# Narrow key tiles of an attention kernel: scores for weights and for maxima of four heads together, in two halves of the same banks

## The chip, the cores and the metric

The kernel runs on one core of one Trainium2 chip. The metric is the device time of one execution in microseconds, as the median of several runs; a profile of one execution is read beside it.

## The reference

The reference is one transformer block on x of 4 x 1024 x 512 (fp32): a layer norm, attention with 16 heads of 32, a layer norm of its output added to x, and then a gated feed-forward net with integer weights, again with a layer norm before and behind it and added.

```python
kqv = x @ Wqkv + bqkv                       # q, k, v: 16 heads of 32
scores = jnp.einsum('bsnh,btnh->bnst', k, q) / math.sqrt(HEAD_SIZE)
ones = jnp.ones_like(scores)
scores = jnp.triu(scores) + -10000.0 * jnp.tril(ones, k=-1)
attn = jax.nn.softmax(scores, axis=2)
out = jnp.einsum('bnkq,bknh->bqnh', attn, v)
out = out.reshape(b, s, NUM_HEADS * HEAD_SIZE)
return out @ Wo + bo

x = x + _layernorm(_L0_attn_ref(_layernorm(x), ...))
x = x + _layernorm(_L0_ffn_ref(_layernorm(x), ...))   # (silu(h Wg) * (h Wu)) Wd
```

For each query the softmax needs a maximum over the keys, the exponentials of the scores less that maximum, their sum, and their product with v.

## The kernel before, in words

The attention stage takes 1250 of the 1980 us; the feed-forward stage (`ffn`) follows and is not touched.

Attention runs in steps (b, hb, g): the batch b of 4, the block hb of four heads, and the half g of 512 queries. A step has 4(g + 1) key tiles of 128 keys. Each key tile c is one period of the main loop, 192 in all, and in a period two things stand side by side:

- `weights(now, c, halves)` makes the scores of 128 keys (the partitions) against the queries that may see them: a product of three rows with ones (L346, it takes the maximum off) and a product of k and q over 32 partitions for each head (L354). ScalarE takes the exponential (L371), POOL sets the diagonal block to zero (L373). The columns n are 512 for most c; in the last key tiles of a step, c = 4g + 1, 4g + 2 and 4g + 3, they are 384, 256 and 128.
- `maxima(unit, jj, k, halves)` makes, for the step that comes 12 periods later (LEAD), the scores of 128 queries (the partitions) against up to 512 keys, over again and the other way round (L265). VectorE limits the diagonal block (L273, "the mask") and takes the maximum (L277, "the reduction"). In the periods with c = 4g + 2 and 4g + 3 these have 256 and 128 columns too.

A half is two heads. A head of 32 takes one of the four groups of 32 rows of the array, so that two heads of weights and the other two heads of maxima run at the same time. That is the order before: in each period, for u = 0 and u = 1, `weights` of half u and `maxima` of half 1 - u.

[...] The pool `ps_st` holds one tile of two banks (one half of weights), `ps_big` is a ring of two tiles of two banks, and `ps_acc` holds `po` and `pd` (outputs and denominators). The ring `ps_big` serves the maxima, and all other work on TensorE that is put between: the projections of q, k and v (`pq`, L237), the output projection (`py`, L237), transposes (`xt` L461, `pv` L488, `pm` L301) and the masked part (`pb` L313). A tile of the ring can be used again when the tile two places before it has been emptied.

Between the two halves of a period stand, on TensorE, `values` of the key tile before (`po` and `pd`, L390) and a piece of other work: `fill_whole` (one of `xt`, `pv`, `pm`, `pb`, where one is due), or else `fill` (one `pq` or `py`). At the end of a period `fill` may add one or more. How much is filled is planned by costs and due times, and the plan is not changed by the edit. Where g = 1, the denominators of the first five key tiles are added up by a DMA that accumulates (L417); `pd` uses the sum in c = 6 and 7.

The order on every engine is the one in which the code issues the instructions (manual_schedule), and waits are set for tiles that are read or written. In the last 12 periods no maxima are left, and `weights` is called with both halves at once; in the first 12 no weights, and `maxima` with both.

```python
pool, tag = (ps_big, "big") if u and len(halves) > 1 else (ps_st, "st")   # weights
...
for u in range(2):                                                        # main loop
    if now and (unit or u == 0):
        weights(*now, [u] if unit else range(2))
    if unit and now:
        maxima(*unit, [1 - u])
```

Of the kernel before, what the change touches and what calls it, by code (L numbers as in the profile page):

```python
# [27 lines left out]
def tile_attn_ffn_sandwich(  # L28
# [70 lines left out]
    with ExitStack() as actx:  # L99
# [143 lines left out]
                    )  # L243


        def maxima(step, jj, k, halves, alone=False):


            b, hb, g = step
            if ("nm", step) not in state:  # L250
                state["nm", step] = e3.tile(
                    [P, 2, 4, HPB], F32, tag="nm", name=f"nm_{b}_{hb}_{g}"
                )
            nm = state["nm", step]
            qT, kT = state["q", b, hb], state["k", b, hb]
            j = 4 * g + jj
            n = min((j + 1) * P - 512 * k, 512)
            for u in halves:
                pool, tag = (ps_st, "st") if alone and u else (ps_big, "big")
                sc = pool.tile(  # L260
                    [P, 2, 512], F32, tag=tag,
                    name=f"sc_{b}_{hb}_{j}_{k}_{u}",
                )
                for h in (2 * u, 2 * u + 1):
                    nc.tensor.matmul(  # L265
                        sc[:, h % 2, :n],
                        lhsT=qT[h * D : (h + 1) * D, ts(j, P)],
                        rhs=kT[h * D : (h + 1) * D, 512 * k : 512 * k + n],
                        start=True,
                        stop=True,  # L270
                    )
                if k == g:
                    nc.vector.tensor_tensor(  # L273
                        sc[:, :, n - P : n], sc[:, :, n - P : n],
                        bound.unsqueeze(1).to_broadcast((P, 2, P)), ALU.min,
                    )
                nc.vector.tensor_reduce(  # L277
                    nm[:, k, jj, 2 * u : 2 * u + 2], sc[:, :, :n], AX.X, ALU.max, negate=True
                )
# [50 lines left out]
            later.extend((counts, shared))  # L330
            state["extra", step] = t1, t2

        def weights(step, c, halves):


            b, hb, g = step
            qT, kT, mT = state["q", b, hb], state["k", b, hb], state["mT", step]
            q0 = max(c * P, 512 * g)
            n = 512 * (g + 1) - q0
            st = {}  # L340
            for u in halves:
                pool, tag = (ps_big, "big") if u and len(halves) > 1 else (ps_st, "st")
                st[u] = pool.tile([P, 2, 512], F32, tag=tag, name=f"st_{b}_{hb}_{g}_{c}_{u}")
            heads = [h for u in halves for h in (2 * u, 2 * u + 1)]
            for h in heads:
                nc.tensor.matmul(  # L346
                    st[h // 2][:, h % 2, :n],
                    lhsT=ones_bf[h * D : h * D + 3, :],
                    rhs=mT[h * D : h * D + 3, 512 - n :],
                    start=True,  # L350
                    stop=False,
                )
            for h in heads:
                nc.tensor.matmul(  # L354
                    st[h // 2][:, h % 2, :n],
                    lhsT=kT[h * D : (h + 1) * D, ts(c, P)],
                    rhs=qT[h * D : (h + 1) * D, q0 : q0 + n],
                    start=False,
                    stop=True,
                )  # L360
            for u in halves:


                to_sum = g > 0 and c == 0
                pT = (p2 if to_sum else ppt).tile(
                    [P, 2, 512], F32, tag="sum" if to_sum else "pT",
                    name=f"pT_{b}_{hb}_{g}_{c}_{u}",
                )
                if to_sum:
                    state["sum", step, u] = pT  # L370
                nc.scalar.activation(pT[:, :, :n], st[u][:, :, :n], AF.Exp)  # L371
                if c >= 4 * g:
                    nc.gpsimd.affine_select(  # L373
                        out=pT[:, :, :P], in_=pT[:, :, :P], compare_op=ALU.is_ge, fill=0.0,
                        base=0, pattern=[[0, 2], [1, P]], channel_multiplier=-1,
                    )
                state["pT", step, c, u] = pT
# [36 lines left out]
        def add_up(step, c, u):  # L414

            if 0 < c <= 4 * step[2]:
                nc.gpsimd.dma_start(  # L417
                    state["sum", step, u], state["pT", step, c, u], accum_op=ALU.add
                )

        def finish(step):
            b, hb, g = step
            if g == 0:
                state["o", b, hb] = (p2 if hb < HC - 1 else p1).tile(
                    [P, S], F32, tag=f"o{hb}", name=f"o_{b}_{hb}"
                )
            o = state["o", b, hb]
            t1, t2 = state.pop(("extra", step))
            nc.vector.tensor_tensor(t2, state["pd"], t2, ALU.add)
            nc.vector.tensor_tensor(t1, state["po"], t1, ALU.add)  # L430

            def divide(k):
                nc.vector.reciprocal(t2[:, ts(k, P)], t2[:, ts(k, P)])  # L433
                nc.gpsimd.tensor_tensor(  # L434
                    o[:, ts(4 * g + k, P)], t1[:, ts(k, P)], t2[:, ts(k, P)], ALU.mult
                )

            for k in range(4):
                later.append(lambda k=k: divide(k))
# [168 lines left out]
        def put(lane, cost, due, ready, f, *args):  # L608
            lane.append((cost, due, ready, f, args))
# [72 lines left out]
        def rate(p):  # L682

            may = sorted(w[:2][::-1] for lane in lanes.values() for w in lane if w[2](p))
            got = total = 0.0
            for due, cost in may:
                total += cost
                got = max(got, total / max(due + 1 - p, 1))

            if p < at[1, 0, 0] - 4:  # L690
                return got
            left = sum(w[0] for lane in lanes.values() for w in lane if w[1] < n_periods)
            return max(got, left / max(n_periods - p, 1))
# [14 lines left out]
        def fill_whole(p):  # L708
            ahead = heads(whole, p)
            if ahead:  # L710
                piece(whole[ahead[0][1]])
            return bool(ahead)
# [21 lines left out]
        for p in range(-LEAD, n_periods + 1):  # L734
            unit = units[p + LEAD] if p + LEAD < len(units) else None
            now = tiles[p] if 0 <= p < n_periods else None
            before = tiles[p - 1] if p >= 1 else None
            spare[0] = max(spare[0], -FULL / 2) + rate(p)
            if rest:
                rest.pop(0)()  # L740
            for u in range(2):
                if now and (unit or u == 0):

                    weights(*now, [u] if unit else range(2))
                if unit and now:
                    maxima(*unit, [1 - u])
                elif unit and u == 0:
                    maxima(*unit, range(2), alone=True)
                if later:
                    later.pop(0)()  # L750
                if before:
                    add_up(*before, u)
                if u == 0:
                    if before:
                        values(*before)
                        if before[1] == 4 * before[0][2] + 3:
                            finish(before[0])

                    if not fill_whole(p) and (
                        not now or now[1] - 4 * now[0][2] > 1 or spare[0] > 1.5 * FULL  # L760
                    ):
                        fill(p, 1)
            if unit and unit[1:] == (0, unit[0][2]):
                shift_parts(unit[0])
                put(whole["rows"], 0, p, lambda q, p=p: q > p, shift_rows, unit[0])
            if now and now[1] == 1:
                put(whole["rows"], 0, p + 1, lambda q, p=p: q > p, masked_part, now[0])
            fill(p, 9)
            if p >= 0 and p % 4 != 3:
                n = next(looks, None)  # L770
                if n is not None:
                    look(n)
            if p > at[B - 1, HC - 1, 0] - LEAD and not pre and not (lanes["qk"] or lanes["v"]):
                ffn_begin()
                for i in range(GT + 1):
                    put(whole["ln"], 0, n_periods, lambda q, t=p + 3 + i: q >= t, ffn_stage, i)
                put(whole["ln"], 0, n_periods, lambda q: True, check_weights)
# [271 lines left out]
```

## Time and profile before

| | |
|---|---|
| median of 3 runs | 1982.24 us (1980.31 to 1984.41) |
| profiled execution | 1981.68 us, span 1979.9 us, granted clock 0.993 |
| TensorE busy | 1888.3 us |
| VectorE busy | 1159.2 us |
| ScalarE busy | 644.2 us |
| POOL busy | 529.3 us |
| L265, scores for maxima | 1536 matmuls, 346.5 us busy |
| L354 and L346, scores for weights | 1536 and 768 matmuls, 307.8 and 125.6 us |
| L277 and L273, maxima and masks | 384 and 256, 367.0 and 109.7 us |
| L371, exponentials | 384, 310.6 us |

Busy times of one line are the union of its instructions, so matmuls that run side by side count once. PE is TensorE, PEld its loading of weights, DVE VectorE, ACT ScalarE. An fp32 matmul of the program shows as two records (two passes), one of bf16 as one. The time that ends in "<-" names what the engine waited for before the instruction.

### The profile page before, as it was taken

Reading aid. Unit: us, or ns where it says so; the run is one execution under the profiler, and the core shown is the slowest. Engines: PE = TensorE matmul, PEld = TensorE weight load, DVE = VectorE, ACT = ScalarE, POOL = GpSimd, SP = SyncE. Lnnn points to the kernel's source line nnn. Section 1 sums busy time; section 2 is a strip of 40 time slices with the busy share of each in tenths; the row PEclk is TensorE's granted clock in tenths of the full one; section 3 lists DMA queues with packets and bytes.
Section 4 is the critical chain, followed back from the end, with each engine's and each line's share of the span. In section 5 each row is a group of like instructions: output and inputs, shape, how many; then the busy total and the mean of one; then the engine's idle time right before and its main releaser. Section 6 shows DMA issues by size and latency. Waiting matters only on the chain.

```text
span 1979.9 us, 42013 instructions
## 1 busy us (share of the span) xinstructions
PE 1888.3 (95%) x18209; PEld 1119.2 (57%) x18209; DVE 1159.2 (59%) x1903; ACT 644.2 (33%) x962; POOL 529.3 (27%) x908
## 2 busy tenths in 40 slices
PE   7999999899999999999999988999999999999997
PEld 4434434444444444444444433688888888888886
DVE  4678767677666676666666773554443444444444
ACT  2234434334333334333344323122222222222221
POOL 2133333243344244244233255201010101101011
PEclk9999999999999999999999999999999999999999
DMA  3163354264154153153244266431010101001000
GB/s 113 54 145 77 85 119 100 67 150 84 36 107 102 34 113 75 34 118 87 38 86 81 82 150 140 156 121 43 1 43 1 43 0 43 27 17 43 1 22 23
DMA packets 66784, 141.74 MB, mean 72 GB/s; under 512 B 6432, under 2 KB 20768, under 8 KB 66592
## 3 DMA queue, kind: packets, MB, share of 16 engines
q0 software_dynamic: 18432, 67.12, 18.2%
q1 hardware_dynamic: 41008, 67.40, 10.2%
q10 hardware_dynamic: 7152, 4.46, 0.8%
q8 instruction: 145, 2.38, 0.5%
q14 instruction: 47, 0.39, 0.1%
HBM read 55.07 MB, written 16.78 MB: 36 GB/s over the span
## 4 chain that ended last, share of the span: by engine, by line
PE 49%; DVE 3%; DMA 2%; POOL 1%; ACT 1%; issue 1%; POOLq 0%; DVEq 0%
PE pg L891 12%; PE pu L891 12%; PE acc L924 12%; PE pq L237 3%; PE py L237 3%; DMA pT<-pT 2%; PE sc L265 2%; PE po L390 1%; PE pd L390 1%; PE st L354 1%; PE st L346 1%; ACT pT L371 1%; DVE nm L277 1%; PE xt L878 1%; POOL xo L520 0%
## 5 line engine op out<-in xcount | busy, mean ns | idle before, releaser
L371 ACT ACTIVATE pT<-st 128x1024 f32<-128x1024 f32 (+3 forms) x384 | 310.6, 811 | 392.6 <-PE st L354 269.2
L277 DVE TENSOR_REDUCE nm<-sc 128x2 f32<-128x1024 f32 (+3 forms) x384 | 367.0, 957 | 107.9 <-PE st L354 88.8
L237 PE MATMUL pq<-xnT,w 128*32 128x256 f32 x6144 | 373.8, 383 | 15.1 <-DVE nm L277 5.8
L265 PE MATMUL sc<-in,in 32*128 32x512 f32 (+3 forms) x1536 | 346.5, 535 | 6.2 <-DVE nm L277 5.9
L237 PEld LDWEIGHTS pq<-xnT,w 128*32 128x32 f32 x6144 | 187.6, 110 | 216.8 <-issue 40.3
L354 PE MATMUL st<-in,in 32*128 32x512 f32 (+3 forms) x1536 | 307.8, 489 | 0.0
L901 DVE SCALAR_TENSOR_TENSOR h<-pu,pre_us,s 128x512 f32<-128x512 f32 x128 | 96.1, 751 | 311.9 <-PE pu L891 309.0
L924 PE MATMUL acc<-d,h 128*128 128x512 f32 x896 | 224.8, 393 | 0.2 <-DVE h L911 0.2
L273 DVE TENSOR_TENSOR sc<-sc,bound 128x256 f32<-128x256 f32 x256 | 109.7, 428 | 189.7 <-PE sc L265 134.1
L373 POOL TENSOR_SCALAR_AFFINE_SELECT pT<-pT 128x256 f32<-128x256 f32 x256 | 108.6, 427 | 320.2 <-ACT pT L371 318.7
L924 PEld LDWEIGHTS acc<-d,h 128*128 128x128 f32 x896 | 166.0, 188 | 34.3 <-DVE h L911 0.5
L899 ACT ACTIVATE s<-pg,pre_gs 128x512 f32<-128x512 f32 x128 | 88.2, 689 | 275.3 <-PE pg L891 275.3
L390 PE MATMUL po<-pT,vt 128*32 128x512 f32 (+3 forms) x1536 | 168.1, 501 | 7.4 <-POOL pT L373 5.9
L910 ACT CAST h<-h 128x512 fp32r<-128x512 f32 x128 | 79.9, 624 | 245.6 <-DVE h L901 245.6
L346 PE MATMUL st<-mT,ones_bf 3*128 3x512 bf16 (+3 forms) x768 | 125.6, 331 | 21.6 <-ACT pT L371 21.2
L434 POOL TENSOR_TENSOR o<-t,t 128x128 f32<-128x128 f32 x128 | 58.6, 458 | 306.6 <-DVE t L433 306.6
L911 DVE TENSOR_TENSOR h<-h,h 128x512 fp32r<-128x512 f32 x128 | 88.7, 693 | 88.3 <-ACT h L910 88.3
L417 POOL DMA_DIRECT2D pT<-pT x128 | 113.7, 888 | 93.4 <-DMA pT<-pT 77.2
L354 PEld LDWEIGHTS st<-in,in 32*128 32x128 f32 x1536 | 134.6, 190 | 1.0
L237 PE MATMUL py<-wo_sb,o 128*32 128x256 f32 x2048 | 126.6, 386 | 8.4 <-POOL o L434 2.6
L346 PEld LDWEIGHTS <-ones_bf 3*128 3x128 bf16 x768 | 40.1, 91 | 160.6 <-issue 156.7
L265 PEld LDWEIGHTS sc<-in,in 32*128 32x128 f32 x1536 | 114.9, 183 | 27.3 <-DVE nm L277 14.8
(131 smaller groups left out, 2479.7 us busy)
## 6 DMA issues: line engine op xcount, KB each, us to landing
pT<-pT POOLq DMA_DIRECT2D x128, 512.0 KB, 5.4
xr<-in_x SPq DMA_DIRECT2D x32, 256.0 KB, 3.3
xo<-in_x SPq DMA_DIRECT2D x32, 256.0 KB, 2.7
x<-xo SPq DMA_DIRECT2D x32, 256.0 KB, 2.0
out<-y SPq DMA_DIRECT2D x32, 256.0 KB, 2.0
look<-in_gate_wt SPq DMA_DIRECT2D x16, 256.0 KB, 3.0
look<-in_up_wt SPq DMA_DIRECT2D x16, 256.0 KB, 3.0
look<-in_down_wt SPq DMA_DIRECT2D x16, 256.0 KB, 3.1
```

What stands on the lines that cost most here:

```text
L237: nc.tensor.matmul(out[k * D : (k + 1) * D, :], lhsT=lhsT[:, k * D : (k + 1) * D], rhs=rhs, start=(c == 0), stop=(c == len(pairs) - 1),)
L265: nc.tensor.matmul(sc[:, h % 2, :n], lhsT=qT[h * D : (h + 1) * D, ts(j, P)], rhs=kT[h * D : (h + 1) * D, 512 * k : 512 * k + n], start=Tru ...
L273: nc.vector.tensor_tensor(sc[:, :, n - P : n], sc[:, :, n - P : n], bound.unsqueeze(1).to_broadcast((P, 2, P)), ALU.min,)
L277: nc.vector.tensor_reduce(nm[:, k, jj, 2 * u : 2 * u + 2], sc[:, :, :n], AX.X, ALU.max, negate=True)
L346: nc.tensor.matmul(st[h // 2][:, h % 2, :n], lhsT=ones_bf[h * D : h * D + 3, :], rhs=mT[h * D : h * D + 3, 512 - n :], start=True, stop=False,
L354: nc.tensor.matmul(st[h // 2][:, h % 2, :n], lhsT=kT[h * D : (h + 1) * D, ts(c, P)], rhs=qT[h * D : (h + 1) * D, q0 : q0 + n], start=False ...
L371: nc.scalar.activation(pT[:, :, :n], st[u][:, :, :n], AF.Exp)
L373: nc.gpsimd.affine_select(out=pT[:, :, :P], in_=pT[:, :, :P], compare_op=ALU.is_ge, fill=0.0, base=0, pattern=[[0, 2], [1, P]], channel_mu ...
L390: nc.tensor.matmul(state[t][h * D : (h + 1) * D, 512 - n :], lhsT=v[:, c, h * D : (h + 1) * D] if t == "po" else ones, rhs=pT[h // 2][:, h ...
L417: nc.gpsimd.dma_start(state["sum", step, u], state["pT", step, c, u], accum_op=ALU.add)
L891: nc.tensor.matmul(dst, lhsT=w[i * P // IB][:, c, ts(i % (IB // P), P)], rhs=part[:, c, :], start=(c == 0 and k == 0), stop=(c == HC - 1 a ...
L924: nc.tensor.matmul(acc[t0][t], lhsT=part[:, ts(t, P)], rhs=dw[i * P // IB][:, i % (IB // P), :], start=(i == 0 and k == 0), stop=(i == IC ...
```

## The change

Where the maxima of a period have no more than 256 columns (a period is then called narrow: `now[1] - 4 * now[0][2] > 1`, with maxima still to make), `weights` is called once, for both halves: half 0 in the tile of `ps_st`, half 1 in one of the ring `ps_big`. It issues the four heads' products for the weights, then calls `maxima` for both halves, which puts its scores into columns 256 to 511 of the same two tiles, issues masks and reductions, and only then come the exponentials. For u = 1 nothing more is issued for scores. `values` and the pieces of other work stand where they stood, behind what is issued for u = 0. In all other periods the order is as before.

```diff
-        def maxima(step, jj, k, halves, alone=False):
+        def maxima(step, jj, k, halves, alone=False, beside=None):
...
+            made = {}
             for u in halves:
+                if beside:
+                    made[u] = beside[u][:, :, 256:]
+                    continue
                 pool, tag = (ps_st, "st") if alone and u else (ps_big, "big")
-                sc = pool.tile(
+                made[u] = pool.tile(
                     [P, 2, 512], F32, tag=tag,
                     name=f"sc_{b}_{hb}_{j}_{k}_{u}",
                 )
+            for u in halves:
+                sc = made[u]
                 for h in (2 * u, 2 * u + 1):
                     nc.tensor.matmul(
...
+            for u in halves:
+                sc = made[u]
                 if k == g:
                     nc.vector.tensor_tensor(
...
-        def weights(step, c, halves):
+        def weights(step, c, halves, unit=None):
...
+            if unit:
+                maxima(*unit, halves, beside=st)
             for u in halves:
...
+            narrow = bool(now and unit and now[1] - 4 * now[0][2] > 1)
             for u in range(2):
-                if now and (unit or u == 0):
+                if narrow:
+                    if u == 0:
+                        weights(*now, range(2), unit)
+                elif now and (unit or u == 0):
                     weights(*now, [u] if unit else range(2))
-                if unit and now:
+                if narrow:
+                    pass
+                elif unit and now:
                     maxima(*unit, [1 - u])
```

## The prediction

> **What bounds the kernel now.** I read the page's engine line first, then the stretches of time, the waits of TensorE, and the timeline of single key tiles.
>
> ```profile
> PE 1888.3 (95%) x18209; PEld 1119.2 (57%) x18209; DVE 1159.2 (59%) x1903; ACT 644.2 (33%) x962; POOL 529.3 (27%) x908
> ```
>
> ```profile
> 300.00:500.00 200.00, 190.23 (x2400) 84.42 (x2395) 143.58 (x225) 79.83 (x117) 72.69 (x127) 0.99 0.45 101
> ```
>
> TensorE is busy 95% over the whole span, and in this 200 us stretch of attention too (its first number, 190.23); VectorE, the third number, is busy 72% there. So a microsecond that TensorE loses in attention is lost at the end, unless a wait for something that has its own clock takes it back. Its waits:
>
> ```profile
> PE st L346 <- ACT pT L371: 21.2, 53, 0.8
> PE pd L390 <- DMA pT<-pT: 14.1, 8, 3.3
> PE sc L265 <- DVE nm L277: 5.9, 6, 2.1
> PE pq L237 <- DVE nm L277: 5.8, 7, 1.1
> ```
>
> Columns: total us, times, longest. Scores for weights wait for the exponential that frees their tile (21.2 us); the denominators pd wait 8 times for the accumulating DMA, which could absorb small shifts just ahead of it. VectorE's maxima are hardly ever waited for, 11.7 us in 13 waits.
>
> Now one key tile that the change touches, g = 0, c = 2 (256 columns), columns start, duration, engine, line:
>
> ```profile
> 523.82 0.28 PE L346 MATMUL st<-mT,ones_bf 3*128 3x256 bf16 x2
> 523.94 0.38 PE L354 MATMUL st<-in,in 32*128 32x256 f32 x2
> 524.16 0.38 PE L354 MATMUL st<-in,in 32*128 32x256 f32 x2
> 524.47 0.85 PE L390 MATMUL po<-pT,vt 128*32 128x384 f32 x8
> 524.65 0.60 ACT L371 ACTIVATE pT<-st 128x512 f32<-128x512 f32 x1 [0.21 <-PE sc L265]
> 524.65 0.43 DVE L273 TENSOR_TENSOR sc<-sc,bound 128x256 f32<-128x256 f32 x1 [0.16 <-PE sc L265]
> 525.12 0.69 DVE L277 TENSOR_REDUCE nm<-sc 128x2 f32<-128x512 f32 x1
> 525.14 0.83 PE L390 MATMUL pd<-pT,ones 128*32 128x384 f32 x8
> 525.90 0.39 PE L313 MATMUL pb<-mT,sel 128*128 128x512 bf16 x1
> 526.22 0.28 PE L346 MATMUL st<-mT,ones_bf 3*128 3x256 bf16 x2
> 527.07 1.93 PE L237 MATMUL pq<-xnT,w 128*32 128x256 f32 x32
> 528.94 0.23 PE L346 MATMUL st<-mT,ones_bf 3*128 3x128 bf16 x2
> ```
>
> From start to start: half a group of scores 0.65, po 0.67, pd 0.76, pb 0.32, the other half 0.85, pq 1.87; together 5.12. The exponential and the masking of the maxima start in the same moment, on two engines: today they do not know of each other.
>
> **What is removed and added.** No instruction goes: as built, the changed kernel has the same 8113 matmuls, the same masks, reductions and exponentials. In 60 of the 192 key tiles (c - 4g > 1 while there are units left: 15 each of g = 0, c = 2 and 3, and g = 1, c = 6 and 7) the two half groups become one: four heads' weights, then four heads' maxima in columns 256 to 511 of the same banks.
>
> *The array's own time.* The trace has four heads' weights in one go, in the last key tiles:
>
> ```profile
> 1220.55 0.29 PE L346 MATMUL st<-mT,ones_bf 3*128 3x256 bf16 x4
> 1220.67 0.60 PE L354 MATMUL st<-in,in 32*128 32x256 f32 x8
> ```
>
> Ones 0.12, as for two heads. Each fp32 product is two passes, 0.22 apart (523.94 to 524.16), and 0.31 pass from the last pass to the next group. So the merged group is 0.12 + 3 x 0.22 + 0.31 = 1.09 us against 0.65 + 0.65 (at 128 columns, where passes are 0.16 apart: 0.45 + 2 x 0.16 = 0.78 against 0.44 + 0.44). That is a gain of 0.21 and 0.10, or 9.3 us over 30 + 30 tiles. Bound below by nothing better than full overlap, which this is; bound above by maxima that load their weights late, as in the run-up (four heads alone, 39.59 to 40.26, 0.67), which would eat the 0.21. I take the gain, since here the load can run under the weights' passes.
>
> *The wait that is added.* As built, the exponential of each half waits for that half's reduction, since both now lie in the same two banks; before, it waits for TensorE alone. Queued behind it on ScalarE are the other half's exponential and the evictions of xt and pq. Who waits: half 1 lies in the "big" ring of two, which xt, pv, pb, pq and py also use. So the second ring tile after it waits for exponential 1. Worked for c = 2, from the group's start:
> - last pass ends at 0.12 + 3 x 0.22 + 0.38 = 1.16; VectorE starts 0.11 later (524.54 to 524.65), at 1.27;
> - mask 0.47, reduce 0.73 (with the 0.04 between them), mask 0.47, reduce 0.69: 3.63;
> - exponential 1: 0.60 and about 0.12 for two handovers: TensorE may go on at 4.35.
> - TensorE itself is there at 1.09 + 0.67 + 0.76 + 0.32 = 2.84, wanting a bank for pq (pb took the other buffer). It stalls 1.51, then pq 1.87: 6.22.
>
> So 6.22 against 5.12: +1.10 each, 15 x 1.10 = +16.5 us. VectorE is idle when the masks come (its 0.16 above), so this is no worst case; where its queue is late by 0.3, it is 1.4 (21 us). What would be the least: handovers of nothing, 1.0 (15 us).
>
> [...]
>
> *g = 0, c = 3* (128 columns; 93.00 to 97.74, 4.74 us). The reduction is 0.42 and the exponential 0.38. Group 0.78; last pass ends at 0.07 + 3 x 0.16 + 0.27 = 0.82; VectorE 0.93 to 2.75; exponential 1 lets go at 3.25. TensorE is there after po 0.45, pd 0.55, pv 0.59, at 2.37: a stall of 0.88, then pq 1.86: 5.11, +0.4. That holds for 12 tiles (those with pv); the 3 without reach the ring late enough, and lose the wait for their last exponential: about -0.5. Sum +3.3.
>
> *g = 1, c = 6* (256 columns). Where xt stands in it (499.28 to 503.91, 4.63 us): 1.09 + po 0.78 + xt 0.59 = 2.46, py needs the bank at 4.35, + 1.87 = 6.22: +1.59, in 7 tiles. With pq or py alone (7 tiles, 4.62) TensorE comes at 3.6 and the next group's half 1 goes on at 4.35: -0.27. One with two py: +0.55. Sum +9.8. But c = 7 follows, where pd waits for the DMA in 8 of 16 steps; what c = 6 loses is there taken back. I take half, +5; ends -1.9 (all losses absorbed) and +9.8.
>
> *g = 1, c = 7* (503.91 to 510.05, 6.14 us): after the group 0.78 stand 2.50 of po and pd, and xt 0.59, so the bank is free (3.87 against 3.25): 3.87 + 1.87 = 5.74, -0.40, 15 x = -6. Its end upward: -2, if only the array's 0.10 is gained.
>
> No DMA, and no SP or POOL work, is moved; POOL's select comes up to 2 us later after its exponential, and is wanted only behind the next merged group. In c = 2 that cover is 6.2 + 0.8 against 4.3 + 0.5 us; gone, it would cost the rest of this chain, no more than the 1.10 again.
>
> Sum: 16.5 + 3.3 + 5 - 6 = +18.8. The profiled execution took 1981.68 us (span 1979.9 and 1.8 around it), 0.56 below the median of the three runs, 1982.24. So 1981.7 + 18.8 = 2000.5, and by the median 2001.
>
> **The rivals.**
> - *Not slower: the merge pays, the wait is covered.* The place is the bank of half 1; it decides if exponential 1 is done before 2.84 us, for which two masks and reductions would have to take 0.85 us in place of 2.36. For it: the 9.3 us of the array and part of the 21.2 us of waits for exponentials go, 1970 us. Against: the rows of VectorE above, and the wait in the build. Chance 0.07.
> - *No difference: the DMA's waits absorb.* pd waits 14.1 us in all; were that all given to the stalls, 18.8 - 14.1 = +4.7, 1986, and less with a lucky c = 2. Against: the 16.5 us of c = 2 come in steps with g = 0, which have no accumulating DMA; the DMAs that follow shift with them. Chance 0.07.
> - *Slower still: late VectorE.* The exponentials hang on VectorE, 72% busy; if its queue is late wherever a mask comes, the upper ends hold: 21 + 5 + 9.8 - 2 = +34, 2016. Chance 0.13.
> - *It does not do what it says*: the merged branch is taken where the two tiles' columns fit 256 + 256; the build shows it 60 times. No chance of its own.
>
> **How the numbers follow.** The forecast, +18.8, has 0.73. Its lower ends: 15 + 1.5 - 1.9 - 6 = +8.6, 1991; its upper as in the third rival. I take 1987 to 2014, which leaves out the first rival, the better part of the second's lower half and the top of the third. 0.2% is 4 us, about what a measurement can tell. Faster 0.07, same 0.07, slower 0.86.
>
> **What would show it.** In the changed profile: pq and py (L237) waiting for ACT pT, some 25 to 35 us in all, in c = 2, c = 3 and c = 6; exponentials of narrow tiles released by DVE nm, not by PE; c = 2 of g = 0 at 6.2 us; c = 7 shorter by 0.4; FFN unchanged. Wrong: if those waits are under 10 us, or c = 2 stays near 5.1.

## The result, and the profile after

The changed kernel takes 2003.32 us (median of 4 runs, 2002.06 to 2009.71), the kernel before 1983.33 us beside it (median of 4 runs, 1980.31 to 1989.36): a ratio of 1.011 with a 95% interval of 1.0084 to 1.0135. That is slower by about 20 us, where +18.8 was forecast. The profiled execution took 2003.45 us with a span of 2001.2 us.

The page's engine line, and TensorE's waits of the changed kernel (total us, times, longest):

```profile
PE 1880.3 (94%) x18209; PEld 1118.3 (56%) x18209; DVE 1168.9 (58%) x1903; ACT 641.0 (32%) x962; POOL 528.9 (26%) x908
```

```profile
PE pq L237 <- ACT pT L382: 27.7, 26, 1.8
PE st L355 <- ACT pT L382: 15.9, 47, 0.8
PE py L237 <- ACT pT L382: 15.0, 11, 1.8
PE pd L401 <- DMA pT<-pT: 13.2, 9, 3.5
PE pm L310 <- DVE wide L302: 6.9, 4, 2.2
```

TensorE is busy 8 us less, which fits the better packing of the merged groups (below), and the span is 21.3 us longer. The new wait stands on top: pq and py wait 42.7 us in 37 places for an exponential, where before they waited 1.2 in one place, by this line of the kernel before:

```profile
PE py L237 <- ACT pT L371: 1.2, 1, 1.2
```

The last line of the changed kernel's list, pm, is new too, and was not forecast.

The same key tile as in the prediction, g = 0, c = 2, in the timeline of the changed kernel (start, duration, engine, line):

```profile
532.17 0.29 PE L355 MATMUL st<-mT,ones_bf 3*128 3x256 bf16 x4
532.72 0.60 PE L272 MATMUL st<-in,in 32*128 32x256 f32 x8
533.25 0.85 PE L401 MATMUL po<-pT,vt 128*32 128x384 f32 x8
533.44 0.43 DVE L282 TENSOR_TENSOR st<-st,bound 128x256 f32<-128x256 f32 x1 [0.60 <-PE st L272]
533.90 0.69 DVE L286 TENSOR_REDUCE nm<-st 128x2 f32<-128x512 f32 x1
534.51 0.42 DVE L282 TENSOR_TENSOR st<-st,bound 128x256 f32<-128x256 f32 x1
534.68 0.39 PE L322 MATMUL pb<-mT,sel 128*128 128x512 bf16 x1
534.71 0.60 ACT L382 ACTIVATE pT<-st 128x512 f32<-128x512 f32 x1 [1.94 <-DVE nm L286]
534.97 0.69 DVE L286 TENSOR_REDUCE nm<-st 128x2 f32<-128x512 f32 x1
535.77 0.60 ACT L382 ACTIVATE pT<-st 128x512 f32<-128x512 f32 x1 [0.47 <-DVE nm L286]
536.42 1.93 PE L237 MATMUL pq<-xnT,w 128*32 128x256 f32 x32 [1.35 <-ACT pT L382]
538.29 0.23 PE L355 MATMUL st<-mT,ones_bf 3*128 3x128 bf16 x4
```

The merged group takes 1.08 us (532.17 to 533.25), where the two half groups were priced at 1.30. Then mask, reduction, mask, reduction stand in a row on VectorE, each exponential follows its reduction, and pq waits for the second one: 1.35 us idle. The period takes 6.12 us; the same one took 5.12.

In attention the trace also has windows, of 3.41 us or twice that, in which TensorE is granted half its clock (0.50 in 288.40 to 291.60, in 622.90 to 626.20 and in 926.70 to 933.30). Adding up, for each place in a step, how much longer its periods are (start of the weights to the next start, all periods of the two traces, us):

| place | in all | without those that a half-clock window touches | such windows, us more |
|---|---|---|---|
| g = 0, c = 2 | +14.1 | +14.1 | 0 |
| g = 0, c = 3 | +0.1 | +0.1 | 0 |
| g = 1, c = 0 | +6.5 | +0.9 | +6.8 |
| g = 1, c = 6 | +4.9 | +0.5 | +5.2 |
| g = 1, c = 7 | -5.1 | -8.7 | +5.0 |
| the rest | +0.8 | +0.8 | +3.4 |
| sum | +21.3 | +7.7 | +20.5 |

The third column is about TensorE's clock: attention has 20.5 us of half clock before and 41.0 us after. The 12 periods that one of these stretches touches, in either trace, lost 13.7 us between them; the 179 others ("clean" below) lost 7.7. Half a clock for 20.5 us more is up to 10 us of work, by estimate. It is not the luck of one trace alone: the mean granted clock was 0.986 to 0.988 in all four runs of the changed kernel, and 0.988 to 0.995 in the 31 runs of the kernel before that stand beside the first experiments.

### The profile page after: what moved, and what is told of

It reads as the page before. It is cut to its first block, busy times and chain, and to the rows that moved or that the text cites. A ratio compares the mean times of both kernels' runs of the same rounds, so it can differ in the third digit from the quotient of the medians.

```text
span 2001.2 us, 41917 instructions
## 1 busy us (share of the span) xinstructions
PE 1880.3 (94%) x18209; PEld 1118.3 (56%) x18209; DVE 1168.9 (58%) x1903; ACT 641.0 (32%) x962; POOL 528.9 (26%) x908
## 4 chain that ended last, share of the span: by engine, by line
PE 48%; DVE 3%; DMA 2%; POOL 1%; ACT 1%; issue 1%; ACTq 0%; POOLq 0%; DVEq 0%
PE pg L909 12%; PE pu L909 12%; PE acc L942 11%; PE pq L237 3%; PE py L237 3%; DMA pT<-pT 2%; PE sc L272 2%; PE st L363 1%; PE po L401 1%; PE st L355 1%; PE pd L401 1%; ACT pT L382 1%; DVE nm L286 1%; PE xt L896 1%; DVE st L282 0%
## 5 line engine op out<-in xcount | busy, mean ns | idle before, releaser
L237 PE MATMUL pq<-xnT,w 128*32 128x256 f32 x6144 | 378.5, 387 | 36.4 <-ACT pT L382 27.7
L286 DVE TENSOR_REDUCE nm<-sc 128x2 f32<-128x1024 f32 (+2 forms) x264 | 299.9, 1137 | 107.4 <-PE st L363 91.8
L272 PE MATMUL sc<-in,in 32*128 32x512 f32 (+2 forms) x1056 | 275.9, 611 | 5.0 <-DVE nm L286 4.7
L363 PE MATMUL st<-in,in 32*128 32x512 f32 (+3 forms) x1536 | 278.5, 491 | 0.0
L928 ACT CAST h<-h 128x512 fp32r<-128x512 f32 x128 | 79.5, 621 | 246.9 <-DVE h L919 246.9
L355 PE MATMUL st<-mT,ones_bf 3*128 3x512 bf16 (+3 forms) x768 | 113.8, 332 | 17.6 <-ACT pT L382 15.9
L79 POOL TENSOR_SCALAR rs_y<-mv_y 128x1 f32<-128x1 f32 x32 | 8.8, 275 | 448.5 <-DVE mv_y L77 448.5
L282 DVE TENSOR_TENSOR sc<-sc,bound 128x256 f32<-128x256 f32 x136 | 58.1, 427 | 115.7 <-PE st L363 64.1
L490 ACT ACTIVATE in<-pq,b_sb 128x256 f32<-128x256 f32 x128 | 60.7, 474 | 189.7 <-PE pq L237 187.7
L444 DVE RECIPROCAL t<-t 128x128 f32<-128x128 f32 x128 | 119.8, 940 | 0.0
```

The lines of the kernel that those rows point to most:

```text
L237: nc.tensor.matmul(out[k * D : (k + 1) * D, :], lhsT=lhsT[:, k * D : (k + 1) * D], rhs=rhs, start=(c == 0), stop=(c == len(pairs) - 1),)
L272: nc.tensor.matmul(sc[:, h % 2, :n], lhsT=qT[h * D : (h + 1) * D, ts(j, P)], rhs=kT[h * D : (h + 1) * D, 512 * k : 512 * k + n], start=Tru ...
L286: nc.vector.tensor_reduce(nm[:, k, jj, 2 * u : 2 * u + 2], sc[:, :, :n], AX.X, ALU.max, negate=True)
L355: nc.tensor.matmul(st[h // 2][:, h % 2, :n], lhsT=ones_bf[h * D : h * D + 3, :], rhs=mT[h * D : h * D + 3, 512 - n :], start=True, stop=False,
L363: nc.tensor.matmul(st[h // 2][:, h % 2, :n], lhsT=kT[h * D : (h + 1) * D, ts(c, P)], rhs=qT[h * D : (h + 1) * D, q0 : q0 + n], start=False ...
```

## The experiments

**One place alone: g = 0, c = 2.** The theory is a chain: the masks and reductions hold the exponentials, these hold the ring tile of half 1, and TensorE wants that tile. The rival is that a merged group costs something wherever it is. Edit (the other two alike, with `now[1] == 3`, and with `now[0][2] == 1`):

```diff
-            narrow = bool(now and unit and now[1] - 4 * now[0][2] > 1)
+            narrow = bool(now and unit and now[1] - 4 * now[0][2] > 1 and now[0][2] == 0 and now[1] == 2)
```

> Only the 15 periods with g = 0, c = 2 are merged, the other 45 are as before. Chain theory (the ring tile of half 1 comes free only after two masks, two reductions and its exponential, and pq wants it): the whole loss of these periods, 15 x 1.0 = +15 us, 1998. Rival, the merge as such costs (four heads at once, the bunched work on VectorE): the loss of 20 us is spread over the 60 merged periods, a quarter of it here, +5 us, 1988.

1994.02 us against 1981.46 for the kernel before on the same chip, ratio 1.0054 (1.0033 to 1.0076). By the ratio +10.7 us, between the two; the rival's 5 is outside the interval (6.5 to 15), the chain's 15 is at its upper end. In its trace c = 2 is longer by 14.1 us, as in the changed kernel, and nothing else by over 2.5; the half-clock stretches are 23.9 us, hardly more than before.

**g = 0, c = 3 alone.**

> Only the 15 periods with g = 0, c = 3 are merged. Chain theory: 12 x 0.2 lost where pv stands before pq, 3 x 0.8 gained where it doesn't, and behind these three the transposes pm may wait for VectorE and give it back and more: between 0 and +6 us, 1983 to 1989. Rival (the merge as such costs): a quarter, +5 us. Nothing lost here would say that a merged period costs nothing unless the ring tile is wanted early.

1990.0 us, ratio 1.0038 (1.0018 to 1.0058): +7.5 us, more than either theory said, though the interval (3.6 to 11.5) holds both, so the total does not decide. The periods c = 3 themselves sum to +0.1 us, as they do in the changed kernel. The loss stands behind them: c = 0 of g = 1 is longer by 7.9 us, where pm waits for VectorE (5.0 us, none before), and c = 7, which is not merged here, by 9.1 us, of which 8.6 are in periods that a half-clock stretch touches; these stretches are 34.1 us in all. So a merged tile that costs nothing itself can cost later.

**g = 1 alone (c = 6 and c = 7).**

> Only the 30 periods with g = 1 (c = 6 and 7) are merged. Chain theory: c = 6 loses where xt stands before py or pq and gains where not, c = 7 gains, and the wait of pd for the DMA takes up much of both: 0 +- 4 us, 1979 to 1987. Rival (the merge as such costs): half of the loss, +10 us, 1993.

1979.07 us, ratio 0.9975 (0.9951 to 0.9998): -5 us, a shade better than before, inside the chain's bounds, and against the rival's +10. The three parts sum to +13 (+10.7 + 7.5 - 5.0), the whole is +22 by its ratio; each part is uncertain by 4 to 5 us, so nothing more than "most of it is g = 0" follows from the sum.

**Swap the tiles of the halves.** Half 0, which is emptied first, goes into the ring.

```diff
-                pool, tag = (ps_big, "big") if u and len(halves) > 1 else (ps_st, "st")
+                ring = u == 0 if unit else u and len(halves) > 1
+                pool, tag = (ps_big, "big") if ring else (ps_st, "st")
```

> All 60 periods merged, but half 0 lies in the ring tile and half 1 in the tile of its own; order and work are the same. Chain theory: the ring tile is free after one mask, one reduction and one exponential, at about 3.17 us from the group's start instead of 4.35, so c = 2 of g = 0 stalls 0.3 instead of 1.5, c = 3 not at all, c = 6 with xt 0.7 instead of 1.9: 20 to 28 us less than the changed kernel, 1975 to 1983. Rival (the merge as such, or VectorE's bunched work, costs): the masks and reductions end at the same time as before the swap, so 2003. Rival clock (the half clock, granted in 12 windows of 3.4 us in attention instead of 6, is the cost): it falls with the stalls only, so the time should follow the count of such windows.

1971.81 us, ratio 0.9944 (0.9925 to 0.9962). The work and its order are the same, only which banks hold which half is not, and the 20 us are gone and 10 more: below the forecast's 1975. TensorE's waits for an exponential, and the lines of the same c = 2:

```profile
PE py L237 <- ACT pT L383: 5.1, 9, 1.2
PE pq L237 <- ACT pT L383: 3.4, 13, 0.7
```

```profile
523.00 0.29 PE L356 MATMUL st<-mT,ones_bf 3*128 3x256 bf16 x4
525.47 0.60 ACT L383 ACTIVATE pT<-st 128x512 f32<-128x512 f32 x1 [1.86 <-DVE nm L286]
526.12 1.93 PE L237 MATMUL pq<-xnT,w 128*32 128x256 f32 x32 [0.21 <-ACT pT L383]
526.54 0.60 ACT L383 ACTIVATE pT<-st 128x512 f32<-128x512 f32 x1 [0.47 <-POOL pT L385]
```

pq goes on 3.12 us after the group's start (forecast 3.17), behind the first exponential; the second starts after it. The 42.7 us of waits are 8.5. This settles the chain against the rival. c = 2 takes 4.99 us at the same place, c = 3 is 8.5 us shorter than before over all steps. The half-clock stretches are 37.5 us here, nearly those of the changed kernel, so the time does not follow them; they cost (pq beside the one at 622.90 of the changed kernel took 4.87 us, in the kernel before 3.66), but are not the cause of the difference between these two.

**Cross the engines.** While ScalarE takes the exponential of half 0, VectorE empties half 1.

```diff
-            for u in halves:
+            for u in reversed(halves) if beside else halves:
                 sc = made[u]
+                if beside and u == 1:
+                    first(0)            # the exponential of half 0
                 ...                     # mask and reduction of half u
+                if beside and u == 1:
+                    first(1)
```

> All 60 periods merged, tiles as in the changed kernel (half 1 in the ring), but the two emptying engines cross: ScalarE takes the exponential of half 0 while VectorE masks and reduces half 1, then they change over. Chain theory: half 1 is free at about 3.2 us from the group's start (reduction 1 ends at 2.47, then its exponential), half 0 at about 3.7, in place of 4.35 and 3.1: the stall of 1.5 us in c = 2 of g = 0 falls to 0.35, as in the swapped kernel, and c = 6 without xt goes on 0.6 earlier than there: 1966 to 1973 us, where before is 1981.5 and the swapped kernel 1972. Rival (the order in which the ring is freed matters no more, VectorE's total does): as the swapped kernel, 1972.

1967.54 us, ratio 0.9928 (0.9903 to 0.9952), the fastest of all. The timeline of the same key tile:

```profile
519.33 0.43 DVE L284 TENSOR_TENSOR st<-st,bound 128x256 f32<-128x256 f32 x1 [0.59 <-PE st L272]
519.33 0.60 ACT L382 ACTIVATE pT<-st 128x512 f32<-128x512 f32 x1 [0.65 <-PE st L272]
519.80 0.69 DVE L288 TENSOR_REDUCE nm<-st 128x2 f32<-128x512 f32 x1
520.60 0.60 ACT L382 ACTIVATE pT<-st 128x512 f32<-128x512 f32 x1 [0.68 <-DVE nm L288]
521.25 1.93 PE L237 MATMUL pq<-xnT,w 128*32 128x256 f32 x32 [0.27 <-ACT pT L382]
```

The two engines start together again, on different halves, and pq waits 0.27 in place of 1.35. The period, 518.07 to 523.12, is 5.05; c = 3 is shorter than before by 0.53 where pv stands in it and by 0.82 where not, c = 6 longer by 0.47 with xt (in three of seven) and shorter by 1.02 without (in five of eight). Against the swapped kernel the intervals overlap; that it is better by these 4 us is likely, not shown.

**Exponentials before the masks.** Both exponentials wait for TensorE alone again, and the masks for them.

> The changed kernel, but both exponentials are issued before the masks, so that they wait for TensorE alone again and the masks wait for them. Chain theory (what counts is when the last of the two engines lets go of the ring tile): mask 0 starts after exponential 0 at 1.9, reduction 1 ends at 4.25 instead of exponential 1 at 4.35: pq stalls as long in c = 2, now for DVE nm instead of ACT pT; 1990 to 2003. Rival (the exponentials being late is the cost, through the weights that are wanted and ScalarE's queue): the loss goes, 1975 to 1983.

1991.48 us, ratio 1.0045 (1.0028 to 1.0063), at the chain's lower end, and not the rival's 1975 to 1983. The edit is `first(0)` and `first(1)` ahead of mask 0, with the halves in their order. Its lines of c = 2:

```profile
528.87 1.08 ACT L381 ACTIVATE pT<-st 128x512 f32<-128x512 f32 x2 [0.65 <-PE st L272]
529.50 0.43 DVE L285 TENSOR_TENSOR st<-st,bound 128x256 f32<-128x256 f32 x1 [1.22 <-ACT pT L381]
531.03 0.69 DVE L289 TENSOR_REDUCE nm<-st 128x2 f32<-128x512 f32 x1
531.87 1.93 PE L237 MATMUL pq<-xnT,w 128*32 128x256 f32 x32 [1.35 <-DVE nm L289]
```

Both exponentials are over at 529.95, early, and pq still waits 1.35 us, for the reduction now. So in c = 2 it does not matter which engine is late, but when the last of the two lets go of the ring tile. c = 2 keeps its loss (+14.9 us, +14.1 in the changed kernel); what falls against the changed kernel, 12 us in all, are c = 6, c = 7 and c = 0 of g = 1, and the half clock (27.3 us for 41.0). Whether the earlier exponentials win something of their own there, as the rival has it, or the clock does, is not separated.

**Double the masks.** Each mask of a merged group is issued twice.

> The changed kernel with every mask of a merged period issued twice (the second changes nothing): 0.47 us more for each half on VectorE, 56 us in all. Chain theory: the ring tile is free 0.94 us later, 15 x 0.94 in c = 2 and 12 x 0.94 in c = 3 of g = 0, and about half of 8 x 0.94 in c = 6: +25 to +35 us over the changed kernel, 2026 to 2036. If VectorE's masks were not on the path, nothing: 2001.

2056.49 us, ratio 1.0369 (1.0325 to 1.0413): +53 us on the changed kernel's 2003 (+51 by the ratios), well over the +25 to +35 that the chain gave. TensorE's waits:

```profile
PE pq L237 <- ACT pT L383: 52.0, 27, 2.7
PE py L237 <- ACT pT L383: 27.5, 15, 2.7
```

The waits grew by 36.8 us (79.5 against 42.7), just over the upper end, and each clean c = 2 by 0.93 to 0.94 where 0.94 was forecast, so VectorE's masks are on the path. The clock can account for the rest: half-clock stretches are 81.9 us in place of 41.0, up to 20 us of work by estimate. With a wait of 1.35 us none of the 15 merged c = 2 periods of the changed kernel met one; here, with 2.3 us, 7 of the 15 did.

**The shift earlier.** In the swapped kernel, `shift_parts` in the merged c = 3 and c = 7 directly behind the reductions.

```diff
                     if u == 0:
                         weights(*now, range(2), unit)
+                        if unit[1:] == (0, unit[0][2]):
+                            shift_parts(unit[0])
...
-                shift_parts(unit[0])
+                if not narrow:
+                    shift_parts(unit[0])
```

> The swapped kernel, and in the merged c = 3 and c = 7 VectorE makes the three parts of the shift right behind the reductions instead of at the period's end, behind the work of the filled pieces. Theory that pm waits because these parts queue behind filled work (pm waits 6.3 us for them in the swapped kernel, 6.9 in the changed one, not at all before): the waits of pm go, and a window of half clock or two with them: 3 to 8 us less than the swapped kernel, 1964 to 1969. Rival (pm is late because VectorE has too much work in all at the step's end): no change, 1972, or a little more, since evictions of the filled work come 1.3 us later.

1984.48 us, ratio 1.0011 (0.9994 to 1.0028): 13 us worse than the swapped kernel, not 3 to 8 better. pm's waits are gone from the list, but pq now waits 6.2 us for the eviction of pv (it didn't in the swapped kernel's list of the longest) and the scores sc 10.4 us for a reduction in place of 4.9. Against the swapped kernel, c = 3 is longer by 7.5 us over all steps and c = 0 of g = 1 by 9.3. VectorE is in arrears there, and what is moved ahead moves something else back.

**pm later.** `shift_rows` let go one period later (`q > p + 1` in place of `q > p`), in three kernels.

> The crossed kernel with the transposes pm (shift_rows) let go one period later, at c = 1 of the next step instead of c = 0; what they make is wanted five or more periods later. Theory that pm's wait for the shift on VectorE (5.5 us in the crossed kernel, none before) gives back what the merged c = 3 wins and costs a half-clock window or two: the first period behind these steps loses its +4 us, 1961 to 1965 against 1967.5. Rival (another wait takes its place, for VectorE is late there in any case): 1967.

> The changed kernel with pm let go one period later, and nothing else. Same theory: c = 0 of g = 1 loses its +6.5 us (pm's 6.9 us of waits and the half clock behind two of them), 1994 to 1999 against 2003. Rival (another wait takes its place): 2001 to 2003.

> The kernel before with pm let go one period later, as a control: pm doesn't wait there, so nothing is won, 1978 to 1984. If it comes down as far as the two others, the gain there has nothing to do with the merge.

1972.31 us (ratio 0.9942, 0.9923 to 0.9961), 2005.7 (1.0114, 1.0082 to 1.0145) and 1988.72 (1.0027, 1.0008 to 1.0046). None got faster, and the control got slower: c = 1 of g = 0 and of g = 1 grow by 9.7 and 4.5 us in the control, as pm pushes other work on, which is more than c = 0 gives back. In the changed kernel pm's wait is gone from the list and c = 0 of g = 1 falls from +6.5 to +1.3 us; but in the control it falls too, by 3.1, so that only some 2 us are left for the first theory. The total is no test of it, since the edit has its own price.

## Why the prediction was right, and where only its sum was

**The wait that was added: right in mechanism, 10% too long.** The forecast for c = 2 was a chain of 4.35 us to pq and a period of 6.22. The trace has 4.25 (532.17 to 536.42) and 6.12; +1.01 in nine of the 15, +0.92 to +0.97 in five, +0.34 in one, so that 16.5 us became 14.1. VectorE started 1.27 us behind the group's start, as forecast (in 12 of the 15; in three 0.2 to 0.3 later). Its four steps ended at 3.49 where 3.63 was forecast, for the second mask starts before the row of the first reduction ends (534.51 against 534.59). The two handovers, charged 0.12, took 0.11 from reduction to exponential and 0.05 to pq. The kernel with the two tiles swapped, the one with exponentials first and the one with doubled masks show that the release of the ring tile is the cause of the loss in c = 2.

**Two engines in one tile.** The forecast had it from the build that an exponential waits for the reduction in its tile, and took the loss to follow from this wait. In the changed kernel the two engines do take turns in one tile, as the exponential at 534.71 shows (ScalarE was idle for 1.94 us before it, until the reduction was done). The crossed kernel has them take turns in the same way, and there it costs next to nothing: 0.27 us of wait. No run here shows what sharing without these waits would do. It was not the sharing as such that cost 20 us, but the order in which the shared tiles were given back.

**c = 3: too large.** +0.4 in 12 tiles and -0.5 in 3 were forecast, +0.21 and -0.82 measured, sum +0.1 for +3.3. The gain of the three was then given back where nothing was expected: behind them pm waits for the shift on VectorE. Two of the three periods there have a half-clock stretch as well and lost 5.6 us; the third lost 0.9.

**c = 6 and c = 7: -0.2 for -1.** With xt +1.45 to +1.55 in four of the five clean cases (+1.59 forecast; the fifth has -0.79); without, -0.84 to -1.03 in six of eight (-0.27 forecast). I had the next group start only when half 1 is free at 4.35; the trace has it start at 3.6 with half 0, and leaves the rest to c = 7. That c = 7 gives or takes by the DMA shows in single steps, written as (c = 6, c = 7): (+1.55, -2.98) in one, (+2.03, -1.24) in another. Single periods c = 7 range from -2.98 to +2.45, so the -0.40 each that the forecast had is not to be seen one by one.

**The clock: missing.** No term of the sum stood for it. Up to 10 of the 21 us are bound up with 20.5 us more of half clock. In the clean periods the loss is 7.7 us, not 18.8: c = 2 and c = 3 were forecast too large by 5 to 6 us together, c = 6 came to +0.5 for +5, and c = 7 got shorter by 8.7, not 6. The periods that a half-clock stretch touches brought the other 13.7. So the agreement of the sum to 2 us is in good part luck; the mechanism of c = 2 is not. Of the signs named beforehand, the exponentials were released by VectorE, c = 2 came to 6.1 and the feed-forward stage did not move. The waits for exponentials, 42.7 us, lie above the 25 to 35 that were named as a sign; the forecast's own stalls (15 of 1.51, 12 of 0.88, 7 of 1.89) add up to 46.

The second rival wanted the waits of pd for the DMA to take up most of the loss; they are 13.2 us in all, 14.1 before. The third rival, VectorE late at the masks, is not what c = 2 shows (0.60 idle before the first mask); where VectorE was late, and no term stood for it, is at pm (6.9 us of waits). The first rival needed the release before 2.84 us from the group's start; in the changed kernel it came at 4.25, in the crossed kernel at 3.18, and there, in another order, the first rival's outcome followed: a merge that pays, at 1967.5 us.

## What to carry to other kernels

When two engines empty one tile in turn, its release is the end of the last of them (here pq went on 4.25 us after the group's start behind the exponential, and 4.26 behind the reduction where the exponentials came first). Put the half that is free first into the buffer that is wanted first (20 us and more here); letting the engines start on different halves and change over did as well. Before putting two results into one bank, work out the time at which its buffer is wanted next, and compare it with the sum of both engines' work, not with each. A gain of TensorE in one period can be spent in the next on a queue of another engine that has not become shorter (here the three periods c = 3 that won 0.82 us each, and the waits of pm for VectorE behind them, 2.19, 2.19 and 0.61 us).

## What the runs showed of the hardware

TensorE waited 1.33 to 1.35 us in each of the 15 merged c = 2 periods of the changed kernel, and none of them has a half-clock stretch; where doubled masks made the same wait 2.3 us, 7 of the 15 have one. The first stretch behind pm began at 622.90, 2.1 us after pm had waited 2.19 us. It lasted 3.41 us, and pq beside it took 4.87 in place of 3.66 us.

```profile
622.90:626.20 3.30, 3.30 (x28) 1.19 (x28) 2.66 (x3) 0.53 (x1) 0.04 (x1) 0.50 0.81 282
```

In this row of the changed kernel's stretches of time the seventh number is the granted clock, 0.50, with TensorE busy throughout. What brings such a stretch about is not shown by these runs.

One thing more can be read from the traces of the changed kernel and of the kernel before: in attention the half-clock stretches begin whole multiples of 3.4133 us apart. In the changed kernel the first three begin at 151.87, 288.40 and 360.08 (40 and 21 times that), in the kernel before the first two at 79.13 and 355.61 (81 times). In the 3.41 us ahead of the stretch at 622.90 TensorE was busy for 2.12 us, ahead of one at 151.87 for 2.31; yet 1.82 us busy, ahead of 814.13, was followed by full clock (three rows; behind the width stands busy TensorE, the clock is the seventh number):

```profile
619.49:622.90 3.41, 2.12 (x14) 0.92 (x14) 3.27 (x9) 1.08 (x2) 2.26 (x4) 1.00 0.21 77
810.72:814.13 3.41, 1.82 (x32) 0.94 (x32) 1.19 (x3) 1.54 (x3) 0.81 (x2) 1.00 0.34 62
814.13:817.54 3.41, 3.41 (x58) 1.68 (x55) 3.13 (x8) 0.38 (x1) 2.17 (x4) 1.00 0.05 17
```

So no single limit on the busy share comes out of these traces.
